# A four-layer network on one core: the rotary part of the query swapped by transfers within SBUF

## The chip, the core and the metric

One Trainium2 chip, one of its cores. The metric is the device time of one execution in microseconds (us); the kernel before was timed three times.

## The reference

Four residual layers over x of shape (4, 512, 1024) in float32: a small attention over the batch, a routed LoRA projection, latent attention with 32 heads, and a second LoRA projection. The change lies in the third. Cut to what matters there:

```python
q = _rmsnorm(x @ wq_a.T, q_a_ln_w) @ wq_b.T            # 32 heads of 64 + 64
q_nope, q_pe = (q[..., :NOPE], q[..., NOPE:])
q_pe = _apply_rope(_deinterleave(q_pe), cos, sin)      # x * cos + rotate_half(x) * sin
k_pe = _apply_rope(_deinterleave(k_pe), cos, sin)
scores = einsum('bqhd,bkhd->bhqk', q_full, k_full) * softmax_scale, causal
out = einsum('bhqk,bkhd->bqhd', softmax(scores), v) @ wo.T
```

`rotate_half` takes the 64 rotary numbers of a head, moves the upper 32 into the place of the lower 32 with a minus sign, and the lower 32 into the place of the upper.

## The kernel before

The heads are worked through as 128 **units**: four groups of eight heads, in each group the four batches, in each batch the eight heads (`units`, L708). A unit has its query transposed: 128 partitions, of which 0 to 63 hold the plain part (with the key's weights already multiplied in) and 64 to 127 the rotary part, by 512 tokens.

Unit u runs through these steps, and the loop at L1214 has several units in work at once:

- `query` (L713): six TensorE matmuls into the PSUM tile `psq` (`po` for the first two units).
- `rotate_query` (L725): ScalarE copies the PSUM tile to `qf` in SBUF (L728). VectorE multiplies the upper 32 rotary partitions of the PSUM tile by the sine into the lower 32 of `t2` (L730), and the lower 32 into the upper 32 (L731). GpSimd multiplies the rotary half of `qf` by the cosine in place (L732), and adds `t2` (L733).
- `split_query` (L736): VectorE rounds 384 tokens of `qf` to the matmul's number format, `qh` (L740), and GpSimd subtracts that from `qf`, `ql` (L741).
- `scores` (L897): for four blocks of queries, TensorE multiplies `qh` and `ql` with the keys into the two PSUM tiles `pss` (L150 to L152 with `ql` first, L912 for the first block), VectorE adds the causal mask and takes the minimum (L918), ScalarE takes the exponential (L921).
- `turn` (L933): TensorE transposes (L942), ScalarE and VectorE copy (L944). `context` (L947): 16 matmuls into `psv` for two units (L958), divided on VectorE (L961) by numbers that `divisors` (L877) sends to DRAM and back: four transfers of 1 KB (L887), two of 64 partitions (L891).
- Between these steps lies filler: `project` (L1007), the output product of the batch before, with its loads (L1020), its splits into two parts (L992 on ScalarE, L993 on GpSimd), its sums (L984, VectorE) and its stores (L1039); and in the first batch of each group `prepare_output` (L1051), which makes the group's output weights (L1068 to L1098).

The query of unit u + 2 is made and rotated in turn u of the loop, split in turn u + 1, used in turn u + 2. All transfers are issued from SyncE's queue (SP), in one order. A planner lays out each engine's order from the program's order and its own estimates; at run time every engine, SP too, works its order strictly in sequence, and an instruction that waits holds those behind it. `qf`, `qh` and `ql` have two buffers each, `t2` has one, `psq` one.

Of the kernel before, what the change touches and what calls it, by code (L numbers as in the profile page):

```python
# [9 lines left out]
F32 = mybir.dt.float32  # L10
FR = mybir.dt.float32r
AF = mybir.ActivationFunctionType
ALU = mybir.AluOpType
# [4 lines left out]
P = 128  # L18
NB, S, D = 4, 512, 1024
# [5 lines left out]
H, NOPE, ROPE, VD, KVR, QR = 32, 64, 64, 128, 64, 256  # L25
# [21 lines left out]
def block_kernel(ctx: ExitStack, tc: tile.TileContext, a: dict, out: bass.AP):  # L47
    nc = tc.nc
    V, A, G, T = nc.vector, nc.scalar, nc.gpsimd, nc.tensor
# [400 lines left out]
    def split_shared(pool, ch):  # L450
# [7 lines left out]
             if kind[0] == "b" and (s or kind == "b11")]  # L458
    w1_d = {(kind, s): dram.tile([P, 2 - ((kind, s) in whole), ND // 2, W1B], F32,
                                 name=f"w1_{kind}{s}") for kind in KINDS for s in range(2)}  # L460
# [48 lines left out]
    with tc.tile_pool(name="b_hTh", bufs=2) as hTh, \  # L509
# [59 lines left out]
        for s, t in enumerate(order):  # L569
# [39 lines left out]
            if s in (10, 11, 12, 13):  # L609
                kind, half = whole[s - 10]  # L610
                row, col = int(kind[1]) - 1, int(kind[2]) - 1
                at = (2 * half + col) * W1B
                with tc.issue_after(kept_x.ins):
                    nc.sync.dma_start(out=w1_d[kind, half][:, 0],
                                      in_=a["w1"][row * ND // 2 : (row + 1) * ND // 2, :, at : at + W1B]
# [26 lines left out]
    cc = attn.enter_context(tc.tile_pool(name="c_const", bufs=1))  # L642
    wqp = attn.enter_context(tc.tile_pool(name="c_wq", bufs=2))
    inp = attn.enter_context(tc.tile_pool(name="c_in", bufs=2))
    qp = attn.enter_context(tc.tile_pool(name="c_q", bufs=2))


    ropeT = cc.tile([P, 2, S], F32, name="ropeT")
    nc.sync.dma_start(out=ropeT[NOPE:P], in_=a["ropeT"])

    causal = cc.tile([P, S], F32, name="causal")
    G.memset(causal, 0.0)
# [58 lines left out]
    lo_, hi_, mid = slice(NOPE, NOPE + 32), slice(NOPE + 32, P), slice(NOPE, P)  # L711
# [13 lines left out]
    def rotate_query(u):  # L725
        ps = queries[u]
        f = qp.tile([P, S], F32, name="qf")
        A.copy(f, ps)  # L728
        t2 = qp.tile([P, S], F32, name="t2", bufs=1)
        V.tensor_tensor(t2[lo_], ps[hi_], ropeT[hi_, 1, :], ALU.mult)  # L730
        V.tensor_tensor(t2[hi_], ps[lo_], ropeT[lo_, 1, :], ALU.mult)  # L731
        G.tensor_tensor(f[mid], f[mid], ropeT[mid, 0, :], ALU.mult)  # L732
        G.tensor_tensor(f[mid], f[mid], t2[mid], ALU.add)  # L733
        queries[u] = f

    def split_query(u):  # L736
# [8 lines left out]
    with tc.tile_pool(name="c1_w", bufs=1, side="right") as wap, \  # L745
# [73 lines left out]
        for s in range(NT + 1):  # L819
            if s < NT:  # L820
                qk[s] = project(s, hts[s])
            if s + 2 < NT:
                hts[s + 2] = turn1(s + 2, ptp)
            if s > 0:
                keep(s - 1, qk[s - 1])
                if order1[s - 1] == TPB - 1:
                    batches[0, 0] = load_batch(0, 0)
            if s in (6, 10):
                wq_raw = fetch_query(s // 4 - 1)
            if s in (8, 12):  # L830
                wqs[s // 4 - 2] = prepare_query(wq_raw, pwp)
            if s in (NT - 2, NT - 1):
                query(s - NT + 2, pwp, "po")
                rotate_query(s - NT + 2)
            if s == NT - 1:
                split_query(0)

                with tc.issue_after(scaled[0].ins):
                    A.activation(first, first, AF.Exp)
# [5 lines left out]
    with ExitStack() as c2:  # L845
# [368 lines left out]
        for u in range(NU + 3):  # L1214
# [37 lines left out]
            if u + 2 < NU:  # L1252
                rotate_query(u + 2)
# [398 lines left out]
def _cos_sin(seq_len, dim=ROPE, base=10000.0, factor=128.0, beta_fast=32.0, beta_slow=1.0,  # L1652
             orig_max=2048):
    import numpy as np

    def corr_dim(r):
        return dim * math.log(orig_max / (r * 2 * math.pi)) / (2 * math.log(base))

    low = max(math.floor(corr_dim(beta_fast)), 0)
    high = min(math.ceil(corr_dim(beta_slow)), dim - 1)  # L1660
    hi = high + 0.001 if low == high else float(high)
    ramp = np.clip((np.arange(dim // 2, dtype=np.float32) - low) / (hi - low), 0.0, 1.0)
    keep = 1.0 - ramp
    extra = 1.0 / base ** (np.arange(0, dim, 2, dtype=np.float32) / dim)
    inter = extra / factor
    inv_freq = inter * (1.0 - keep) + extra * keep
    freqs = np.outer(np.arange(seq_len, dtype=np.float32), inv_freq)
    emb = np.concatenate([freqs, freqs], axis=-1)
    return np.cos(emb).astype(np.float32), np.sin(emb).astype(np.float32)


def _laid_out(i):

    import numpy as np

    even_odd = np.concatenate([np.arange(0, ROPE, 2), np.arange(1, ROPE, 2)])
    half = ROPE // 2
    cos, sin = _cos_sin(S)
    by_tile = lambda t: t.reshape(TPB, P, ROPE).transpose(1, 0, 2)
    signed = np.concatenate([-sin[:, :half], sin[:, half:]], axis=1)  # L1680

    signed_T = np.concatenate([sin[:, :half], -sin[:, half:]], axis=1)
    wkv_a = i["L1_attn_wkv_a"]
    wq_b = i["L1_attn_wq_b"].reshape(H, NOPE + ROPE, QR)
    wkv_b = i["L1_attn_wkv_b"].reshape(H, NOPE + VD, KVR)
    chunks = lambda w: w.T.reshape(ND, P, -1)
    lora_in = lambda w: w.reshape(ER, D)
    lora_out = lambda w: w.transpose(0, 2, 1).reshape(ER, D)
    return {
        "x": i["L0_attn_x"].reshape(NB * S, D),  # L1690
        "w0": chunks(np.concatenate([lora_in(i["L0_ffn_A"]), i["L0_ffn_W_gate"], i["L0_ffn_W_base"]])),
        "b0T": lora_out(i["L0_ffn_B"]),
        "b0": i["L0_ffn_b_base"],
        "waT": chunks(np.concatenate([i["L1_attn_wq_a"], wkv_a[:KVR], wkv_a[KVR:][even_odd]])),
        "q_ln": i["L1_attn_q_a_ln_w"],
        "kv_ln": i["L1_attn_kv_a_ln_w"],
        "wqn": wq_b[:, :NOPE].transpose(1, 0, 2),
        "wqpT": wq_b[:, NOPE:][:, even_odd].transpose(2, 0, 1).reshape(2, P, H, ROPE).transpose(1, 0, 2, 3),
        "wk": wkv_b[:, :NOPE].transpose(1, 0, 2),
        "wv": wkv_b[:, NOPE:].transpose(1, 0, 2),  # L1700
        "woT": i["L1_attn_wo"].T.reshape(H, VD, D),
        "w1": chunks(np.concatenate([i["L1_ffn_W"][:W1B], lora_in(i["L1_ffn_A"]), i["L1_ffn_W"][W1B:]])),
        "b1T": lora_out(i["L1_ffn_B"]),
        "b1": i["L1_ffn_b"],
        "rwT": i["L1_ffn_router_W"].reshape(E, ND, P).transpose(2, 0, 1),
        "rb": i["L1_ffn_router_b"],
        "ropeN": np.stack([by_tile(cos), by_tile(signed)], axis=1),
        "ropeT": np.stack([cos.T, signed_T.T], axis=1),
    }


# [18 lines left out]
```

## Time and profile before

| what | value |
|---|---|
| median of three runs | 1747.93 us (1747.41 to 1749.18) |
| span of the profiled execution | 1746.3 us |
| the stage of the heads in it | about 414 to 1480 us |
| granted TensorE clock, mean | 0.999 |
| ScalarE busy | 905.0 us (52%) |
| L728, copy of the query from PSUM, 126 of 128 | 73.9 us, 587 ns each |
| L730 and L731, 32 x 512, 126 of 128 | 87.7 and 87.1 us, 696 and 691 ns each |
| L732 and L733, 64 x 512, 128 each | 164.4 and 164.3 us, 1285 and 1284 ns each |
| transfers, mean over the span | 131 GB/s, 39.2% of the 16 DMA engines |

Busy time is that of the whole span. The times of the runs lie 1.6 us above the span, since a run has a little before its first instruction and after its last. Line numbers are those of the kernel before.

### The profile page before, as it was taken

What the parts mean: (1) busy time and instruction counts of PE and PEld (TensorE: products, weight loads), DVE (VectorE), ACT (ScalarE), POOL (GpSimd) and SP (SyncE); (2) the same over time, 40 slices, a digit from 0 to 9 for tenths busy, and PEclk for the clock granted to TensorE, in tenths of its full rate; (3) what the DMA queues carried; (4) which work ended last, traced back from release to release, by engine and by line L of the source; (5) the groups of instructions that cost most, each with busy time, mean ns of one, the idle gap of its engine ahead of it and who ended that gap; (6) DMA issues with size and microseconds to landing.
All of it is one profiled execution on the core that took longest, in us unless ns stands there. A gap on an engine that the chain in (4) does not pass through costs nothing.

```text
span 1746.3 us, 31628 instructions
## 1 busy us (share of the span) xinstructions
PE 1707.5 (98%) x10536; PEld 1429.7 (82%) x10536; DVE 1302.4 (75%) x3494; ACT 905.0 (52%) x2316; POOL 921.9 (53%) x926
## 2 busy tenths in 40 slices
PE   7999999999999999999999999999999999999999
PEld 6899999998677777767777767777767777789998
DVE  7977885676777777787777687777778776687675
ACT  7422331366765555575555575555476555453332
POOL 0553541203665665566566556566556655675454
PEclk9999999999999999999999999999999999999999
DMA  4313543245334234353333353342454333853431
GB/s 194 135 42 115 185 159 114 89 138 169 106 99 140 81 118 140 113 172 117 110 112 119 110 193 95 106 139 94 131 169 151 102 110 109 309 201 123 137 105 74
DMA packets 131939, 228.16 MB, mean 131 GB/s; under 512 B 22272, under 2 KB 58752, under 8 KB 128448
## 3 DMA queue, kind: packets, MB, share of 16 engines
q1 hardware_dynamic: 131776, 226.13, 39.2%
q8 instruction: 84, 1.38, 0.3%
q14 instruction: 79, 0.65, 0.1%
HBM read 156.60 MB, written 71.83 MB: 131 GB/s over the span
## 4 chain that ended last, share of the span: by engine, by line
PE 88%; DVE 5%; POOL 4%; ACT 2%; issue 1%; DMA 0%; POOLq 0%; ACTq 0%; DVEq 0%
PE psv L958 8%; PE pst L942 7%; PE po L150 4%; PE po L152 4%; PE po L151 4%; PE pss L150 4%; PE pss L151 3%; PE pss L152 3%; PE pob L150 3%; PE poa L150 3%; PE psq L150 3%; PE psq L152 3%; PE psq L151 3%; PE acc L150 3%; PE acc L152 3%; PE acc L151 3%
## 5 line engine op out<-in xcount | busy, mean ns | idle before, releaser
L921 ACT ACTIVATE p<-p,mn 128x512 f32<-128x512 f32 (+3 forms) x512 | 284.9, 559 | 211.4 <-DVE mn L918 210.8
L732 POOL TENSOR_TENSOR qf<-qf,ropeT 64x512 f32<-64x512 f32 x128 | 164.4, 1285 | 259.1 <-ACT qf L728 249.3
L918 DVE CUSTOM_DVE_ANT_0 p<-pss,causal 128x512 f32<-128x512 f32 (+3 forms) x512 | 232.7, 485 | 19.8 <-PE pss L152 15.8
L942 PE MATMUL pst<-ident,p 128*128 128x128 f32 x1280 | 185.9, 273 | 1.8 <-ACT pT L944 1.7
L733 POOL TENSOR_TENSOR qf<-qf,t 64x512 f32<-64x512 f32 x128 | 164.3, 1284 | 32.0 <-DVE t L731 23.8
L942 PEld LDWEIGHTS pst<-ident,p 128*128 128x128 f32 x1280 | 153.0, 141 | 29.6 <-ACT pT L944 4.8
L944 ACT COPY pT<-pst 128x512 f32<-128x512 f32 x256 | 142.1, 579 | 31.4 <-PE pst L942 29.5
L741 POOL TENSOR_TENSOR ql<-qf,qh 128x384 fp32r<-128x384 f32 x128 | 129.6, 1013 | 53.0 <-DVE qh L740 53.0
L150 PE MATMUL pss<-kT,ql 128*128 128x512 f32 (+2 forms) x384 | 143.6, 374 | 4.4 <-POOL ql L741 4.2
L993 POOL TENSOR_TENSOR cxl<-s,cxh 128x256 fp32r<-128x256 f32 x128 | 98.1, 773 | 85.2 <-ACT cxh L992 53.9
L150 PE MATMUL po<-w_h,hTl 128*128 128x384 f32 (+1 forms) x384 | 133.1, 347 | 0.7 <-DVE x L433 0.6
L151 PE MATMUL pss<-kT,qh 128*128 128x512 f32 (+2 forms) x384 | 130.4, 340 | 0.0
L152 PE MATMUL po<-w_h,hTh 128*128 128x384 f32 (+1 forms) x384 | 130.1, 339 | 0.0
L152 PE MATMUL pss<-kT,qh 128*128 128x512 f32 (+2 forms) x384 | 129.9, 338 | 0.0
L151 PE MATMUL po<-w_l,hTh 128*128 128x384 f32 (+1 forms) x384 | 129.7, 338 | 0.0
L944 DVE COPY pT<-pst 128x256 f32<-128x256 f32 x128 | 54.1, 423 | 97.8 <-PE pst L942 97.2
L728 ACT COPY qf<-psq 128x512 f32<-128x512 f32 x126 | 73.9, 587 | 69.7 <-PE psq L152 68.0
L730 DVE TENSOR_TENSOR t<-psq,ropeT 32x512 f32<-32x512 f32 x126 | 87.7, 696 | 24.5 <-ACT qf L728 20.2
L921 ACT ACTIVATION_READ_ACCUMULATOR p<-p,mn 128x1 f32 x512 | 97.2, 190 | 0.0
L150 PEld LDWEIGHTS pss<-kT,ql 128*128 128x128 f32 x384 | 72.1, 188 | 29.1 <-POOL ql L741 9.2
L731 DVE TENSOR_TENSOR t<-psq,ropeT 32x512 f32<-32x512 f32 x126 | 87.1, 691 | 1.7
L1035 DVE TENSOR_TENSOR xs<-xs,pob 128x512 f32<-128x512 f32 x105 | 71.1, 677 | 19.0 <-PE pob L152 18.8
(567 smaller groups left out, 4975.0 us busy)
## 6 DMA issues: line engine op xcount, KB each, us to landing
xs<-x_d SPq DMA_DIRECT2D x128, 256.0 KB
x_d<-xs SPq DMA_DIRECT2D x128, 256.0 KB
slotC<-in_woT_dram SPq DMA_DIRECT2D x32, 512.0 KB
rb<-r_d SPq DMA_DIRECT2D x128, 128.0 KB
w_t<-raw SPq DMA_DIRECT2D x32, 288.0 KB
x<-in_x_dram SPq DMA_DIRECT2D x16, 512.0 KB
x_d<-x SPq DMA_DIRECT2D x32, 256.0 KB
slotA<-q_d SPq DMA_DIRECT2D x8, 1024.0 KB
```

Source lines behind the costliest of these rows:

```text
L150: T.matmul(ps, lhsT=al, rhs=bh, start=start, stop=False, **kw)
L151: T.matmul(ps, lhsT=ah, rhs=bl, start=False, stop=False, **kw)
L152: T.matmul(ps, lhsT=ah, rhs=bh, start=False, stop=stop, **kw)
L732: G.tensor_tensor(f[mid], f[mid], ropeT[mid, 0, :], ALU.mult)
L733: G.tensor_tensor(f[mid], f[mid], t2[mid], ALU.add)
L741: G.tensor_tensor(l, f[:, P:S], f32(h), ALU.subtract)
L918: turn_of[0] = V.tensor_tensor_reduce(out=to, in0=ps[:, 0:n], in1=causal[:, S - n : S], scale=1.0, scalar=-NEG, op0=ALU.add, op1=ALU.min, ...
L921: A.activation(to, to, AF.Exp, bias=mn[:, i : i + 1], scale=-1.0, accum_out=rs[:, i : i + 1])
L942: T.transpose(ps[:, w : w + P], p[:, OF[i] + j * P : OF[i] + (j + 1) * P], ident)
L944: copy(pT[:, AT[js[0]] : AT[js[0]] + w], ps[:, 0:w])
L958: T.matmul(ps[n * KVR : (n + 1) * KVR, S - w : S], lhsT=k[:, j, :], rhs=pTs[u + n][:, AT[j] : AT[j] + w], start=(j == 0), stop=(j == TPB - 1))
L993: G.tensor_tensor(l, src, f32(h), ALU.subtract)
```

## The change

The query's rotary half is rotated from SBUF. After ScalarE's copy, two transfers carry 32 partitions by 512 numbers each (64 KB) of `qf` into partitions 0 to 63 of `t2`, crosswise. VectorE multiplies these 64 partitions by the signed sine in one instruction, into partitions 64 to 127 of `t2`. GpSimd multiplies by the cosine into a tile of its own, `tc`, and adds. The table `ropeT` has the signed sine in partitions 0 to 63 and the cosine in 64 to 127, 2 KB a partition where it had 4 KB in half the partitions.

```diff
-    ropeT = cc.tile([P, 2, S], F32, name="ropeT")
-    nc.sync.dma_start(out=ropeT[NOPE:P], in_=a["ropeT"])
+    ropeT = cc.tile([P, S], F32, name="ropeT")
+    nc.sync.dma_start(out=ropeT, in_=a["ropeT"])
...
         A.copy(f, ps)
         t2 = qp.tile([P, S], F32, name="t2", bufs=1)
-        V.tensor_tensor(t2[lo_], ps[hi_], ropeT[hi_, 1, :], ALU.mult)
-        V.tensor_tensor(t2[hi_], ps[lo_], ropeT[lo_, 1, :], ALU.mult)
-        G.tensor_tensor(f[mid], f[mid], ropeT[mid, 0, :], ALU.mult)
-        G.tensor_tensor(f[mid], f[mid], t2[mid], ALU.add)
+        nc.sync.dma_start(out=t2[0:32], in_=f[hi_])
+        nc.sync.dma_start(out=t2[32:NOPE], in_=f[lo_])
+        V.tensor_tensor(t2[mid], t2[0:NOPE], ropeT[0:NOPE], ALU.mult)
+        tc_ = qp.tile([P, S], F32, name="tc", bufs=1)
+        G.tensor_tensor(tc_[mid], f[mid], ropeT[mid], ALU.mult)
+        G.tensor_tensor(f[mid], tc_[mid], t2[mid], ALU.add)
         queries[u] = f
...
-    signed_T = np.concatenate([sin[:, :half], -sin[:, half:]], axis=1)
...
-        "ropeT": np.stack([cos.T, signed_T.T], axis=1),
+        "ropeT": np.concatenate([signed.T, cos.T]),
```

## The prediction

> **What bounds the kernel now.** I read the page first, then the busy time by stretches, then the timeline unit by unit, last the waits.
>
> ```profile
> PE 1707.5 (98%) x10536; PEld 1429.7 (82%) x10536; DVE 1302.4 (75%) x3494; ACT 905.0 (52%) x2316; POOL 921.9 (53%) x926
> ...
> DMA  4313543245334234353333353342454333853431
> ...
> PE 88%; DVE 5%; POOL 4%; ACT 2%; issue 1%; DMA 0%; POOLq 0%; ACTq 0%; DVEq 0%
> ```
>
> TensorE (PE) is busy all along and makes 88% of the chain that ended last. VectorE and GpSimd (POOL) hold 5% and 4% of it, 87 and 70 us: places, not the whole.
>
> ```profile
> 414.00:500.00 86.00, 80.87 (x445) 56.11 (x444) 67.00 (x197) 61.67 (x167) 55.19 (x49) 1.00 0.45 145
> 500.00:620.00 120.00, 120.00 (x675) 94.32 (x674) 87.76 (x242) 67.59 (x189) 71.93 (x71) 1.00 0.31 101
> ```
>
> Columns: stretch, its length, busy PE, weight loads, VectorE, ScalarE, POOL, clock, share of the DMA engines, GB/s. In the steady stretch TensorE has no idle time at a clock of 1.00: shorter work elsewhere can give nothing back there, a late operand can only take. The start of the heads has 5 us of idle TensorE in 86.
>
> How late may the operand come? One unit, from its query to its score:
>
> ```profile
> 608.99 0.59 ACT L728 COPY qf<-psq 128x512 f32<-128x512 f32 x1 [0.53 <-PE psq L152]
> ...
> 609.67 0.70 DVE L730 TENSOR_TENSOR t<-psq,ropeT 32x512 f32<-32x512 f32 x1
> 609.72 1.28 POOL L732 TENSOR_TENSOR qf<-qf,ropeT 64x512 f32<-64x512 f32 x1 [0.70 <-ACT qf L728]
> ...
> 610.38 0.69 DVE L731 TENSOR_TENSOR t<-psq,ropeT 32x512 f32<-32x512 f32 x1
> ...
> 611.21 1.28 POOL L733 TENSOR_TENSOR qf<-qf,t 64x512 f32<-64x512 f32 x1 [0.21 <-DVE t L731]
> ...
> 612.52 0.36 DVE L740 CAST qh<-qf 128x384 fp32r<-128x384 f32 x1 [0.25 <-POOL qf L733]
> ...
> 612.96 1.01 POOL L741 TENSOR_TENSOR ql<-qf,qh 128x384 fp32r<-128x384 f32 x1 [0.47 <-DVE qh L740]
> ```
>
> The copy ends at 609.58 (call it E), the two multiplications end at E + 1.49, the cosine at E + 1.42, the addition runs from E + 1.63 to E + 2.91, `ql` is done at 613.97. In the timeline the first weight load of this unit's scores comes at 617.27: 3.3 us to spare. The unit before it has nothing to spare:
>
> ```profile
> 608.01 1.01 POOL L741 TENSOR_TENSOR ql<-qf,qh 128x384 fp32r<-128x384 f32 x1
> ...
> 609.07 0.19 PEld L150 LDWEIGHTS pss<-kT,ql 128*128 128x128 f32 x1
> ```
>
> Reading all 128 units so, from the end of L741 to that weight load, I count 39 units with under 0.35 us, 16 with 0.35 to 1.3, 15 with 1.3 to 2.4, 58 with more. The 39 are of two kinds. Some 20 lie in the steady stretch, as the one above: its addition ended at 604.57, but L740 had its turn on VectorE only at 606.31 and L741 its turn on POOL, behind three L993, at 608.01; so 1.7 us of lateness vanish before L741, except what the L993 between are pushed. The other 19 lie in the start of the heads (units 0 to 11) and in the three later stretches of `prepare_output`, with the addition, L740, L741 and the scores end to end. The waits say the same in sum:
>
> ```profile
> PEld pss L150 <- POOL ql L741: 9.2, 23, 1.5
> ```
>
> **The change, part by part.** *VectorE:* 128 x (0.696 + 0.691) = 177 us go, and one multiplication over 64 partitions comes. Its price is not in the trace; nearest is L984, two SBUF inputs, 128 x 512:
>
> ```profile
> L984 DVE TENSOR_TENSOR s<-a,a x16: 679/811/1328, 1506.8 to 1718.0; 128x512 f32<-128x512 f32 x16
> ```
>
> So 0.68 to 1.33 us; I take 0.75, as POOL has mostly just ended the cosine. The spread comes from POOL, as this pair shows (another L984, 128 x 256, takes 0.41 undisturbed at 605.38):
>
> ```profile
> 757.66 1.01 POOL L741 TENSOR_TENSOR ql<-qf,qh 128x384 fp32r<-128x384 f32 x1 [0.47 <-DVE qh L740]
> ```
>
> ```profile
> 757.84 1.10 DVE L984 TENSOR_TENSOR s<-cx 128x256 f32<-128x256 f32 x1
> ```
>
> The removed multiplications read PSUM and never stretch (695 to 697 ns in all 128). The Trainium skill ("SBUF — State Buffer", section "SBUF: two separate sides") has here an exclusive lock: a VectorE operation with two SBUF inputs and a GpSimd operation that reads SBUF each hold the other out for the whole instruction. The row ends 0.27 us after POOL's, less than a full 0.41, so the lock is not quite that strict; by the rule a multiplication that meets a whole GpSimd operation would cost 0.69 + 1.28 = 1.97 us, an estimate, and such a meeting alone would make its unit's lateness 2.5 where I take 1.3.
>
> VectorE is thus relieved by 128 x (1.387 - 0.75) = 82 us of busy time. I cost this at nothing, because the steady stretch is TensorE's; where VectorE is on the chain it is a gain, in the rivals. `psq` comes free when the copy ends, 1.4 us earlier; TensorE waited for that once, 0.5 us.
>
> *Transfers:* 256 of 64 KB, 16.8 MB on 226 MB, 7%: not the bandwidth. What counts is issue and landing, and the trace shows no transfer within SBUF. Nearest are the four of 1 KB to DRAM, whose landing the next two wait for:
>
> ```profile
> 599.82 1.30 SPq L887 DMA_DIRECT2D r_d<-rt  x4
> ...
> 602.54 1.09 SPq L891 DMA_DIRECT2D rb<-r_d  x2
> ```
>
> An issue costs 1.30 / 4 = 0.33 us, and from the end of the last issue (601.12) to 602.54 are 1.42 us. So the second swap is issued by E + 0.05 + 0.66 and has landed at E + 2.1 with a free queue. Bounds: 0.7 less if a landing within SBUF takes half; and more when it waits its turn: SP gives 1.30 + 1.09 us to the divisors every second unit, and loads wait on SP for earlier transfers with all behind them held:
>
> ```profile
> SPq L1020 <- DMA x_d<-xs: 61.9, 60, 3.4
> ```
>
> or when the 16 engines still work off 1 MB of loads (a load of 256 KB at the steady 101 GB/s over a share of 0.31, some 325 GB/s, takes 0.8 us, four 3.2). The Trainium skill ("DMA: Bandwidth & Descriptors", section "Anatomy of one DMA") gives 2.0 us plus the bytes over 436 GB/s, for GpSimd's path: 2.15 us for 64 KB, and its rules for kernel authors advise against small transfers and against halving one by partitions. By it, as an estimate, landing is at E + 2.9 and every shift below is 0.8 larger, some 36 us more in the sum; I hold to the row, which is of the same queue.
>
> *POOL:* same two operations of 1.28 us; the new tile changes no wait, since only POOL touches it before the addition. `ropeT` is the same 256 KB once: nothing.
>
> *The shift.* Multiplication from E + 2.1 to E + 2.85, addition from E + 2.9 where it was E + 1.6: **1.3 us later** (0.6 with the quick landing; 1.9 with the stretched multiplication; 2.4 to 3.0 behind the divisors' issues or loads).
>
> *What 1.3 us costs.* I move each addition in the timeline, push POOL's operations behind it, L740 and L741 as far as needed, and count what comes after the scores' weight load. The 19 tight units pay 0.1 to 1.3, 0.55 in the mean (several have 0.3 to 1.7 us between addition and L740): 10 us. The 20 steady ones pay what the L993 were pushed, 0.2: 4 us. All others have room. Sum 14 us for an unhindered transfer. The same count gives 27 us at a shift of 1.6, 41 at 1.9, 66 at 2.4, 105 at 3.0, and 3 at 0.7. For hindered transfers I add 5 us: about one unit in eight meets a queue of a further 1.1 us and pays some 0.3 of it beyond its slack, 16 x 0.3.
>
> VectorE's multiplication itself waits for the transfer. Behind it stand L918, the copies L944 and L740, hence ScalarE's exponential and TensorE's transposes. I cost that wait at nothing because VectorE idles 32 of 120 us in the steady stretch, 2 us a unit, if the planner sets the multiplication at its due time; where it does not, that is the first rival. Swaps waiting on SP for the copy hold `r_d` and loads behind them for well under 1 us; `rb` is due some 8 us later.
>
> Sum: span 1746.3 + 14 + 5 - 1 (VectorE's relief, `psq`) = 1764.3; the median stands 1.6 above the span: **1766 us**. The likeliest case's own range, shifts of 1.0 to 2.1 (6 to 50 us): 1754 to 1798.
>
> **The rivals.** *Late transfers block VectorE.* SP's order and the load queue bring a swap 3 us late in the mean and VectorE stands in front of L918. For: SP's waits, the DMA slices at 4 to 8 tenths; against: at 3 tenths most swaps meet a free queue. By the count, 105 us: 1853; it decides from a mean landing of E + 3.8, and half as much (2.4, 66 us) still ends at 1814.
>
> *The lateness is hidden.* The planner sees the transfer and moves the filler of `project` ahead of the scores, so that tight units stop being tight. For: 73 of 128 units have over 1.3 us; against: the start has little filler and the tight places are bound by POOL. Then only some 2 us remain: 1749.
>
> *VectorE's relief wins.* In the start of the heads the chain of waits gives 3.2% of 86 us to L731 and about 2% to L730; 0.64 us less a unit for the 45 or so units outside the steady stretch, at a third of them on the chain, is 10 us: 1738. It decides if a swap lands before E + 0.7, since the addition is then no later; half the row's landing and a joined issue would be needed. Against: 1.42 us for 1 KB.
>
> *The change does not do what it says:* a multiplication stretched to 1.33 by POOL leaves VectorE as busy as before (1.39); that is the shift of 1.9 above, inside the forecast.
>
> **How the numbers follow.** Forecast 0.58, blocked VectorE 0.16, hidden 0.13, relief 0.13. A measurement tells 0.2% (3.5 us) from no change. Slower holds the first two, 0.74; the hidden case is the same, 0.13; relief faster, 0.13. From 1743 to 1805 leaves about 0.1 out below and 0.1 above.
>
> **What would show it.** After: the addition starts 2.9 us behind the copy's end, not 1.6; `pss` weight loads wait for `ql` some 25 us in sum, not 9; the new multiplication lasts 0.69 alone and longer beside POOL; TensorE's work is the same with more idle time between 414 and 500 and in the three stretches of `prepare_output`. I am wrong if TensorE's idle time sits in front of transposes (late exponentials: blocked VectorE), or if the addition comes no later.

## The result, and the profile after

| kernel | median, range | ratio to before, 95% interval |
|---|---|---|
| before | 1748.33 us (1747.41 to 1749.18) | |
| after | 1925.66 us (1923.63 to 1929.21) | 1.1015 [1.1002, 1.1029] |

The change costs 177 us. The prediction had the side right and the size wrong: 1766 us, with a range that ended at 1805.

From the page of the kernel after, the busy time of the engines, TensorE's (PE) share and its granted clock by slices, and the groups of VectorE's mask instruction (L920), of the scores' first matmuls (L150), of the addition (L735), of the new multiplication (L732) and of the context's division (L963) (behind the bar: mean ns of one, then idle time in front of the group and what ended it):

```profile
PE 1751.6 (91%) x10536; PEld 1452.1 (75%) x10536; DVE 1236.4 (64%) x3366; ACT 908.3 (47%) x2316; POOL 932.9 (48%) x926
...
PE   7999999998888999978999978999997988989999
...
PEclk9999999999899999989999999999998999999999
...
L920 DVE CUSTOM_DVE_ANT_0 p<-pss,causal 128x512 f32<-128x512 f32 (+3 forms) x512 | 234.7, 488 | 189.8 <-PE pss L152 177.4
L150 PE MATMUL pss<-kT,ql 128*128 128x512 f32 (+2 forms) x384 | 150.5, 392 | 136.7 <-POOL ql L743 136.6
L735 POOL TENSOR_TENSOR qf<-tc,t 64x512 f32<-64x512 f32 x128 | 164.6, 1286 | 148.3 <-DVE t L732 79.0
...
L732 DVE TENSOR_TENSOR t<-t,ropeT 64x512 f32<-64x512 f32 x128 | 106.3, 831 | 16.9 <-DMA t<-qf 13.3
...
L963 DVE TENSOR_TENSOR cx<-psv,rb 128x512 f32<-128x512 f32 x64 | 44.2, 691 | 79.1 <-PE psv L960 71.9
```

TensorE has the same 10536 matmuls, and where it was busy 98% of the span it is busy 91%. VectorE (DVE) has 66 us less to do, as the change means it to, and that is worth nothing. The main cause stands in the line of L150: 136.6 us in which TensorE waits for `ql`, the last product of the query's chain (4.2 before). The addition, further up that chain, waits 79.0 us for the multiplication; this is GpSimd's idle time and no further part of the loss.

The span grew by 178 us: TensorE is idle 134 us longer, and it is also busy 44 us longer (1707.5 before) with the same matmuls. The granted clock shows where part of the 44 comes from. In the slices it is 9 all through before; here it is 8 in three of them, and its mean is 0.983 where it was 0.999. By the clock's records 68 us of the span run at half clock (5 before), and TensorE is busy in 54 of them (3 before): some 26 us more work time, as an estimate. The remaining 18 are not broken down. What lowers the clock no run shows by itself; the runs with much idle time on TensorE have it (of the runs below, 39 us at half clock in `unread`, 67 in `order`), those with little have not (2 in `unread_const`, 5 in `deep_swap`). So the prices below hold TensorE's waits and the lower clock together.

The stretches that the prediction showed, of the kernel after (same columns):

```profile
414.00:500.00 86.00, 70.02 (x342) 47.52 (x341) 43.32 (x141) 48.18 (x130) 38.98 (x34) 0.94 0.41 124
500.00:620.00 120.00, 105.56 (x572) 79.18 (x571) 71.24 (x199) 60.63 (x169) 65.85 (x63) 0.99 0.33 102
```

The steady stretch, 120.00 of 120 before, now has 14 us of idle TensorE. All but some 3 us of the loss is in the heads: the first copy of a query ends at 415.2 us (414.6 before), and from the last copy to the end it is 280.4 us (277.8).

One unit in the timeline of the kernel after, from its copy to its scores (start, length; the copy ends at 641.82, which is E):

```profile
641.23 0.59 ACT L728 COPY qf<-psq 128x512 f32<-128x512 f32 x1 [0.69 <-POOL ql L743]
...
642.30 0.51 SPq L730 DMA_DIRECT2D t<-qf  x1
...
642.86 0.59 SPq L731 DMA_DIRECT2D t<-qf  x1
...
645.32 0.69 DVE L1037 TENSOR_TENSOR xs<-xs,pob 128x512 f32<-128x512 f32 x1 [0.34 <-PE pob L152]
...
645.93 0.42 DVE L920 CUSTOM_DVE_ANT_0 p<-pss,causal 128x256 f32<-128x256 f32 x1
...
646.38 1.14 DVE L732 TENSOR_TENSOR t<-t,ropeT 64x512 f32<-64x512 f32 x1
...
647.65 1.29 POOL L735 TENSOR_TENSOR qf<-tc,t 64x512 f32<-64x512 f32 x1 [0.68 <-POOL cxl L995]
...
649.41 0.99 POOL L743 TENSOR_TENSOR ql<-qf,qh 128x384 fp32r<-128x384 f32 x1 [0.47 <-DVE qh L742]
...
650.46 0.50 PE L150 MATMUL pss<-kT,ql 128*128 128x512 f32 x1 [1.43 <-POOL ql L743]
```

SyncE (SP) starts the first swap 0.48 us behind the copy, since it is still issuing the divisors' transfers; the two issues last 0.51 and 0.59 us; the second swap's semaphore moves at 644.84 (E + 3.0). VectorE doesn't take up the multiplication then: two instructions stand ahead of it, and the first of them waits for TensorE (0.34 us). The multiplication starts at E + 4.6, the addition at E + 5.8, and TensorE stands 1.43 us in front of the scores.

Over all 128 units (means from the instructions' own times):

| behind the copy's end | predicted | measured, mean (median) |
|---|---|---|
| first swap's issue starts | 0.05 | 1.02 (0.25) |
| second swap's issue ends | 0.71 | 2.29 (1.64) |
| both have landed | 2.1 | 3.95 (3.28) |
| multiplication starts | 2.1 | 6.07 (5.40) |
| addition starts | 2.9 | 7.28 (6.32) |

Between the landing and the multiplication lie 2.1 us in the mean, 271 us over all units. In these VectorE works 142 us and stands idle for 129, 118 of them in front of instructions that wait for TensorE, the divisions of L963 (57 us) and L920 (50) above all. So TensorE's own lateness comes back through VectorE's order: late scores make those instructions late, and they hold the next multiplication.

Before, the addition started at 1.84 (1.58). Units with under 0.35 us between `ql` and the scores' weight load were 39; they are 117.

### The profile page after: what moved, and what is told of

Read it like the earlier page. It is cut to its first block, busy times and chain, and to the rows that moved or that the text cites. A ratio compares the mean times of both kernels' runs of the same rounds, so it can differ in the third digit from the quotient of the medians.

```text
span 1924.4 us, 32100 instructions
## 1 busy us (share of the span) xinstructions
PE 1751.6 (91%) x10536; PEld 1452.1 (75%) x10536; DVE 1236.4 (64%) x3366; ACT 908.3 (47%) x2316; POOL 932.9 (48%) x926
## 5 line engine op out<-in xcount | busy, mean ns | idle before, releaser
L920 DVE CUSTOM_DVE_ANT_0 p<-pss,causal 128x512 f32<-128x512 f32 (+3 forms) x512 | 234.7, 488 | 189.8 <-PE pss L152 177.4
L150 PE MATMUL pss<-kT,ql 128*128 128x512 f32 (+2 forms) x384 | 150.5, 392 | 136.7 <-POOL ql L743 136.6
L735 POOL TENSOR_TENSOR qf<-tc,t 64x512 f32<-64x512 f32 x128 | 164.6, 1286 | 148.3 <-DVE t L732 79.0
L150 PEld LDWEIGHTS pss<-kT,ql 128*128 128x128 f32 x384 | 75.9, 198 | 183.6 <-POOL ql L743 166.4
L734 POOL TENSOR_TENSOR tc<-qf,ropeT 64x512 f32<-64x512 f32 x128 | 167.7, 1310 | 80.5 <-ACT qf L728 74.3
L995 POOL TENSOR_TENSOR cxl<-cx,cxh 128x256 fp32r<-128x256 f32 x96 | 72.2, 755 | 140.4 <-ACT cxh L994 137.9
L151 PE MATMUL pss<-kT,qh 128*128 128x512 f32 (+2 forms) x384 | 136.4, 355 | 0.0
L152 PE MATMUL pss<-kT,qh 128*128 128x512 f32 (+2 forms) x384 | 135.7, 353 | 0.0
L150 PE MATMUL po<-w_h,hTl 128*128 128x384 f32 (+1 forms) x384 | 133.0, 346 | 0.2 <-DVE x L433 0.2
L742 DVE CAST qh<-qf 128x384 fp32r<-128x384 f32 x128 | 46.1, 360 | 127.6 <-POOL qf L735 127.6
L732 DVE TENSOR_TENSOR t<-t,ropeT 64x512 f32<-64x512 f32 x128 | 106.3, 831 | 16.9 <-DMA t<-qf 13.3
L963 DVE TENSOR_TENSOR cx<-psv,rb 128x512 f32<-128x512 f32 x64 | 44.2, 691 | 79.1 <-PE psv L960 71.9
```

The costliest lines, as they stand in the source:

```text
L150: T.matmul(ps, lhsT=al, rhs=bh, start=start, stop=False, **kw)
L151: T.matmul(ps, lhsT=ah, rhs=bl, start=False, stop=False, **kw)
L152: T.matmul(ps, lhsT=ah, rhs=bh, start=False, stop=stop, **kw)
L732: V.tensor_tensor(t2[mid], t2[0:NOPE], ropeT[0:NOPE], ALU.mult)
L734: G.tensor_tensor(tc_[mid], f[mid], ropeT[mid], ALU.mult)
L735: G.tensor_tensor(f[mid], tc_[mid], t2[mid], ALU.add)
```

## The experiments

The theory after the result: the loss is the lateness of the addition; it comes from SP's queue, from the issues, and from the place that the multiplication has in VectorE's order. The rivals: the transfers' own traffic, the hold-up between VectorE's multiplication, which now reads SBUF alone, and GpSimd, and a VectorE that stands waiting for transfers. Unless said otherwise a diff is against the kernel after.

**Are the transfers as such the cost?** Two runs keep both transfers and take VectorE's products from PSUM again. In `unread` the transfers land where nobody reads them, though GpSimd's addition, which writes into `qf`, still has to wait until they have read it:

```diff
-        V.tensor_tensor(t2[mid], t2[0:NOPE], ropeT[0:NOPE], ALU.mult)
+        V.tensor_tensor(t2[lo_], ps[hi_], ropeT[0:32], ALU.mult)
+        V.tensor_tensor(t2[hi_], ps[lo_], ropeT[32:NOPE], ALU.mult)
```

> The changed kernel with its transfers kept, but nobody waits for them: they land in partitions 0 to 63 of t2, which nothing reads, and VectorE makes the two products from PSUM as before (the cosine product stays in its own tile). Theory A, lateness (the rotated query reaches the scores late, since the addition starts 7.3 us behind the copy in the mean instead of some 1.9): 1748 to 1760 us, the addition back under 2.5 us behind the copy. Theory B, load (256 more transfers on the one queue and the DMA engines hold up others): 1800 us or more.

Measured: 1843.64 us, ratio 1.054 [1.0525, 1.0556]; the addition starts at 4.51 (us behind the copy's end, mean, as all such numbers below). From the waits of `unread` (time in all, number, longest):

```profile
POOL qf L736 <- DMA t<-qf: 63.5, 40, 4.6
...
PE pss L150 <- POOL ql L744: 57.5, 46, 5.2
```

The addition still waits for a transfer, and TensorE for the addition's chain. So this run did not free the chain, and it can't price the traffic. In `unread_const` the transfers read the constant table in place of `qf`:

```diff
-        nc.sync.dma_start(out=t2[0:32], in_=f[hi_])
-        nc.sync.dma_start(out=t2[32:NOPE], in_=f[lo_])
+        nc.sync.dma_start(out=t2[0:32], in_=ropeT[hi_])
+        nc.sync.dma_start(out=t2[32:NOPE], in_=ropeT[lo_])
```

(with VectorE's two lines as in `unread`)

> Like the run unread, but the 256 transfers read the constant rope table instead of qf, so that nothing waits for them at all (in unread the addition into qf still waited until the transfers had read it); both products from PSUM. Traffic and issues on SP alone. If they cost by themselves: 1775 us or more. If the cost is the lateness of the addition: 1748 to 1760 us, the addition under 2.5 us behind the copy.

Measured: 1756.95 us, 1.0054 [1.004, 1.0068]; addition at 1.86. The same 256 transfers of 64 KB, issued from the same queue, cost 9 us when nothing waits for them. The traffic falls as a cause of 177 us. One thing this run leaves out: its transfers read a constant, so they are issued 5.5 us ahead of the copy's end in the mean and SP never stands for a copy. In the change SP does:

```profile
SPq L730 <- ACT qf L728: 185.1, 69, 8.1
SPq L889 <- DVE rt L885: 137.9, 34, 9.0
```

The loads and stores behind such a wait are held. In the change TensorE's own waits for loads in the heads are 1.2 us in sum, and VectorE's for `rb` 6.8, so little of the loss lies there. `act_queue` below takes the swaps off SP.

**The multiplication alone, without transfers.** `no_transfer` multiplies `qf` in SBUF straight on; `psum64` multiplies the PSUM tile. Both leave out the swap of the halves and take the cosine for the sine.

```diff
-        nc.sync.dma_start(out=t2[0:32], in_=f[hi_])
-        nc.sync.dma_start(out=t2[32:NOPE], in_=f[lo_])
-        V.tensor_tensor(t2[mid], t2[0:NOPE], ropeT[0:NOPE], ALU.mult)
+        V.tensor_tensor(t2[mid], f[mid], ropeT[mid], ALU.mult)
```

> The changed kernel without its two transfers: one product over 64 partitions from SBUF, of the rows as they stand (the swap of the halves is left out). Theory A: 1740 to 1752 us, as the product follows the copy at once; VectorE has 0.7 us less a unit. Theory C, the product from SBUF costs by itself, since it and GpSimd hold each other up: 1770 us or more, with the product well over 0.83 us in the mean.

Measured: 1780.6 us, 1.0176 [1.0159, 1.0193].

In `psum64` the added line is:

```diff
+        V.tensor_tensor(t2[mid], ps[mid], ropeT[mid], ALU.mult)
```

> Like the run no_transfer (one product over 64 partitions, halves not swapped, no transfer), but the product reads PSUM instead of qf, so that only one of its inputs is in SBUF. If the 31 us of no_transfer come from VectorE and GpSimd holding each other up: 1742 to 1752 us, with the cosine product at 1.28 us where it was 1.72. If they come from another order of the work or from the separate cosine tile: 1770 to 1785 us again.

Measured: 1747.27 us, 0.9996 [0.9986, 1.0005]. VectorE is relieved by some 0.69 us a unit, 88 us in sum, and the kernel doesn't move: the relief is worth nothing here. And one operand from SBUF in place of PSUM costs 33 us. The timeline of `no_transfer` shows how:

```profile
849.75 0.69 DVE L730 TENSOR_TENSOR t<-qf,ropeT 64x512 f32<-64x512 f32 x1
849.86 1.72 POOL L732 TENSOR_TENSOR tc<-qf,ropeT 64x512 f32<-64x512 f32 x1 [1.85 <-ACT qf L728]
```

GpSimd's (POOL) cosine product starts beside VectorE's and lasts 1.72 us; its mean is 1.68 here and 1.29 in `psum64`. In the 107 units where VectorE starts first and undisturbed, its product still has 0.59 us to run when GpSimd's starts, and GpSimd's is 0.46 us longer. From the waits of `no_transfer`:

```profile
PE pob L150 <- POOL cxl L993: 12.1, 14, 1.6
PE poa L150 <- POOL cxl L993: 10.3, 13, 0.9
```

TensorE waits 22.4 us for GpSimd's other work, the low parts `cxl` of the output product's operand, 3.7 us before (2.9 and 0.8) and 1.9 in `psum64`. So most of this loss, some 20 of the 33 us, goes by GpSimd's time and not by the query, whose addition starts at 2.11. The kernel after hardly has it: there the multiplication comes when the cosine product is long done, that one lasts 1310 ns in the mean, and TensorE's waits for `cxl` stay at 3.5 us. So hardly any of the 33 us is in the 177.

**Which part of the lateness?** `act_queue` issues the transfers from ScalarE's own queue, right behind the copy:

```diff
-        nc.sync.dma_start(out=t2[0:32], in_=f[hi_])
-        nc.sync.dma_start(out=t2[32:NOPE], in_=f[lo_])
+        nc.scalar.dma_start(out=t2[0:32], in_=f[hi_])
+        nc.scalar.dma_start(out=t2[32:NOPE], in_=f[lo_])
```

> The changed kernel with the two transfers issued from ScalarE's queue, right behind the copy, instead of SP's. If SP's order holds the swaps up (first issue 1.0 us behind the copy in the mean, up to 9.7): 1870 to 1910 us, with issues right behind the copy. If ScalarE's own issues (256 of some 0.55 us) put the exponentials late: 1930 us or more.

Measured: 1887.75 us, 1.0811 [1.0779, 1.0843]. The first issue starts at 0.14 (1.02 in the change), the landing is at 3.58, the addition at 6.03. 38 us of the 177 come back, so SP's order is not the main part. Nor are the 38 its price alone: the landing is only 0.4 us earlier, and 0.9 us of the addition's 1.25 come from a shorter stand of the multiplication behind the landing (1.2 us for 2.1), while ScalarE now spends 0.58 us on each of the 256 issues. `one_transfer` moves the 64 partitions in one piece, its halves not swapped:

```diff
-        nc.sync.dma_start(out=t2[0:32], in_=f[hi_])
-        nc.sync.dma_start(out=t2[32:NOPE], in_=f[lo_])
+        nc.sync.dma_start(out=t2[0:NOPE], in_=f[mid])
```

> The changed kernel with one transfer of 64 partitions by 512 in place of two of 32 (the swap of the halves is left out). If the second issue on SP (0.55 to 0.59 us) and its semaphore are a share: landing some 0.6 us earlier, the addition 0.6 to 1.3 us earlier, 1885 to 1910 us. If the landing and the order alone set it: 1915 to 1930 us.

Measured: 1883.8 us, 1.0775 [1.076, 1.079]; landing at 3.38, addition at 5.79. One transfer in place of two is worth 42 us, again by two ways: the landing is 0.6 us earlier, and the multiplication stands 1.15 us behind it in place of 2.1. `swap_product` lets VectorE multiply from PSUM at once (the table's sine is signed for the place that the product goes to), and swaps the product's halves afterwards, so that only GpSimd's addition waits for a transfer:

```diff
-        nc.sync.dma_start(out=t2[0:32], in_=f[hi_])
-        nc.sync.dma_start(out=t2[32:NOPE], in_=f[lo_])
-        V.tensor_tensor(t2[mid], t2[0:NOPE], ropeT[0:NOPE], ALU.mult)
-        tc_ = qp.tile([P, S], F32, name="tc", bufs=1)
-        G.tensor_tensor(tc_[mid], f[mid], ropeT[mid], ALU.mult)
-        G.tensor_tensor(f[mid], tc_[mid], t2[mid], ALU.add)
+        V.tensor_tensor(t2[mid], ps[mid], ropeT[0:NOPE], ALU.mult)
+        t3 = qp.tile([P, S], F32, name="t3", bufs=1)
+        nc.sync.dma_start(out=t3[lo_], in_=t2[hi_])
+        nc.sync.dma_start(out=t3[hi_], in_=t2[lo_])
+        G.tensor_tensor(f[mid], f[mid], ropeT[mid], ALU.mult)
+        G.tensor_tensor(f[mid], f[mid], t3[mid], ALU.add)
```

> One product over 64 partitions straight from PSUM behind the copy (sine signed for the place that it goes to), then the two transfers swap the halves of the product, and GpSimd adds what has landed: correct rotation, no VectorE operation behind the transfer, no two SBUF inputs on VectorE, the cosine product in place. If the place of the product in VectorE's order (2.1 us behind the landing in the mean) is a share of the loss: the addition at 3.5 to 4.8 us behind the copy and, at some 30 us per us of lateness, 1800 to 1850 us. If whatever comes behind a transfer is set so late on its engine, GpSimd too: the addition at 6 us or more, 1880 to 1930 us.

Measured: 1855.65 us, 1.0616 [1.0602, 1.0631]. The landing is later than in the change, 4.55, because the multiplication comes first; still the addition is earlier, 5.90, and 70 us come back. A transfer behind the multiplication is cheaper than one ahead of it. `order` tried the place itself: VectorE's context and filler of the next turn were put behind the multiplication (`turned_q[0]` is that instruction).

```diff
-            advance(cx)
-            advance(filler, per[0])
+            with tc.issue_after(turned_q[0].ins):
+                advance(cx)
+                advance(filler, per[0])
```

> The changed kernel, with the next turn's context and filler work on VectorE queued behind the rotary product, so that the product stands earlier in VectorE's order. Of theory A, if the place in the order (2.1 us behind the landing in the mean) is the larger share: the product within 1 us of the landing, the addition some 1.5 to 2 us earlier, 1830 to 1880 us. If the transfer's own 3 us are the share that counts: 1900 to 1940 us, and VectorE waits for the transfer in front of the product.

Measured: 1954.49 us, 1.1173 [1.1154, 1.1193]: a miss, and slower than the change. The multiplication still starts 2.0 us behind the landing in the mean (2.1 in the change), the addition at 6.97, and the work that was put behind it is late as well (TensorE waits 11.7 us for the sums `xs` of the output product, 0.4 in the change). The edit moved other work without moving the multiplication much, so it says nothing of what a better place would bring.

**A longer lead.** `deep_after` makes the query three units ahead in place of two. Room for a third `qf` comes from one of five `xs` tiles and one of two `junk` tiles.

```diff
-        f = qp.tile([P, S], F32, name="qf")
+        f = qp.tile([P, S], F32, name="qf", bufs=3)
...
-            if 0 < u < NU - 2:
-                query(u + 2, psq, "psq")
-            if u + 2 < NU:
-                rotate_query(u + 2)
+            if 0 < u < NU - 3:
+                query(u + 3, psq, "psq")
+            if u + 3 < NU:
+                rotate_query(u + 3)
```

> The changed kernel, transfers and all, but the query of unit u + 3 instead of u + 2 is made and rotated in turn u, with a third buffer for qf (room for it: four instead of five xs tiles, one junk tile): some 8 us more between rotation and split. Theory A: most of the 177 us come back, 1750 to 1790 us, with TensorE's wait for ql under 60 us in sum where it was 303. Theory B or C: no less than 1880 us, since load and lock stay the same.

Measured: 1773.26 us, 1.0136 [1.0121, 1.0151]. The addition starts at 6.95, nearly as late as in the change, and yet 152 of the 177 us are gone; 20 units are tight in place of 117, and the clock is at half for 14 us in place of 68. The multiplication stands 1.2 us behind the landing in place of 2.1, though `rotate_query` stands at the same place of the loop. So the lateness is paid only where a unit has no slack for it. The same lead on the kernel before is `deep_before`:

> The kernel before with the same deeper lead as deep_after (query of u + 3, three qf buffers, four xs tiles, one junk tile). Control of deep_after: what it lies below 1773 us is the change's own cost when there is time for it. If the 20 or so units before that had nothing to spare cost anything: 1735 to 1745 us; if the smaller room costs: 1750 to 1765 us.

Measured: 1746.12 us, 0.9989 [0.998, 0.9999]. The lead itself gives almost nothing, for the kernel before has little lateness to hide.

What are the 27 us that `deep_after` lies above `deep_before`? The theory then was the hold-up of `no_transfer`. Three runs with the longer lead (`deep_no_transfer` and `deep_swap_sbuf` take the cosine for the sine, and the first leaves out the swap): `deep_swap` is `swap_product` with it, `deep_no_transfer` is `no_transfer` with it, and `deep_swap_sbuf` is `deep_after` with these lines:

```diff
-        nc.sync.dma_start(out=t2[0:32], in_=f[hi_])
-        nc.sync.dma_start(out=t2[32:NOPE], in_=f[lo_])
-        V.tensor_tensor(t2[mid], t2[0:NOPE], ropeT[0:NOPE], ALU.mult)
+        V.tensor_tensor(t2[0:NOPE], f[mid], ropeT[mid], ALU.mult)
+        nc.sync.dma_start(out=t2[lo_], in_=t2[32:NOPE])
+        nc.sync.dma_start(out=t2[hi_], in_=t2[0:32])
```

> The longer lead of deep_after (the query three units ahead, three qf buffers, four xs tiles, one junk buffer) with the rotation of swap_product: VectorE multiplies all 64 partitions from PSUM, where the product shares no lock with GpSimd (psum64: no loss), and two transfers then swap the product's halves before GpSimd's addition. It asks what the 27 us are that deep_after still lies above deep_before. If they are the hold-up between VectorE's product from SBUF and GpSimd's cosine product (no_transfer against psum64: 31 us), this run is at 1750 to 1760: deep_before and the 9 us that the transfers cost by themselves in unread_const. If they are lateness that three units of lead don't cover, or the transfers' own load, it is at 1768 or above, as deep_after is at 1773. In both cases far below swap_product (1856), and the addition still starts 5 to 6 us behind the copy's end.

Measured: 1748.26 us, 1.000 [0.999, 1.001], a little under the hold-up theory's own number.

> no_transfer with the longer lead of deep_after: VectorE's one product reads qf in SBUF beside GpSimd's cosine product, nothing waits for a transfer. It leaves out the swap of the halves and multiplies by the cosine in place of the sine. If the 27 us that deep_after lies above deep_before come from the hold-up between VectorE's product from SBUF and GpSimd, as deep_swap's 1748 suggests, they are here too: 1765 to 1780. If the longer lead covers the hold-up as it covers deep_swap's transfers, because 0.44 us a unit are small against a median slack of some 8 us, it is at 1746 to 1752, and the 27 us belong to the place that VectorE's product has behind a transfer.

Measured: 1746.9 us, 0.9986 [0.9977, 0.9996], though the cosine product still lasts 1.67 us in the mean. The theory falls: with this lead the hold-up costs nothing.

> deep_swap with VectorE's product taken from qf in SBUF in place of PSUM (and GpSimd's cosine product into a tile of its own, as in the change); the two transfers swap the product's halves as there. It multiplies by the cosine in place of the sine. Hold-up theory: deep_swap and some 25 us, 1768 to 1780. Theory of VectorE's product queued behind a transfer: it isn't queued behind one here, so 1748 to 1755, as deep_swap.

Measured: 1770.87 us, 1.0122 [1.0105, 1.0139]. By its number this run would speak for the hold-up; its waits show something else as well. TensorE's waits in the heads, of `deep_after`, then `deep_swap`, then `deep_swap_sbuf`:

```profile
PE pss L150 <- POOL ql L743: 27.3, 15, 3.4
```

```profile
PE pss L150 <- POOL ql L743: 4.9, 6, 1.1
```

```profile
PE pss L914 <- DVE mn L920: 7.9, 5, 2.4
PE pss L150 <- DVE mn L920: 7.3, 8, 1.2
PE pss L150 <- POOL ql L743: 6.7, 6, 1.5
PE pob L150 <- DVE xs L1037: 6.1, 5, 1.4
```

and VectorE's own wait in front of its multiplication in `deep_swap_sbuf`:

```profile
DVE t L730 <- POOL qf L735: 15.3, 11, 2.4
```

In `deep_after` it is `ql` again, 27.3 us in 15 waits: single units with more lateness than even this lead covers. In `deep_swap` that has shrunk to 4.9. `deep_swap_sbuf` waits for VectorE instead, and it has an edit too many: product and swapped product share the one buffer of `t2`, so that VectorE's multiplication stood 15.3 us for GpSimd's addition of the unit before, with VectorE's other work behind it. That wait is new; how much of the 23 us is its own and how much the hold-up's was not taken apart.

**The version that beats both.** `deep_table` is the kernel before with the longer lead and with the packed table of the change, whose 2 KB a partition leave room for all five `xs` tiles (the diff is against the kernel before):

```diff
-        V.tensor_tensor(t2[lo_], ps[hi_], ropeT[hi_, 1, :], ALU.mult)
-        V.tensor_tensor(t2[hi_], ps[lo_], ropeT[lo_, 1, :], ALU.mult)
-        G.tensor_tensor(f[mid], f[mid], ropeT[mid, 0, :], ALU.mult)
+        V.tensor_tensor(t2[lo_], ps[hi_], ropeT[0:32], ALU.mult)
+        V.tensor_tensor(t2[hi_], ps[lo_], ropeT[32:NOPE], ALU.mult)
+        G.tensor_tensor(f[mid], f[mid], ropeT[mid], ALU.mult)
```

> The kernel before with the deeper lead, but all five xs tiles: the rope table is packed as in the changed kernel (sine in partitions 0 to 63, read beside PSUM rows 64 to 127), which makes room for the third qf buffer. Rotation from PSUM, no transfer. If the units that before had nothing to spare cost something that the four xs tiles of deep_before took back: 1736 to 1744 us. If TensorE's own work is all there is to it: 1745 to 1750 us.

Measured: 1742.27 us (1739.27 to 1746.4), 0.9964 [0.9953, 0.9975]: 6 us faster than the kernel before, with no transfers.

## Why the prediction was wrong

**The failed step is the shift of the addition**, "1.3 us later". Measured it is 7.28 - 1.84 = 5.4 us in the mean. Its pieces, which are not independent, since lateness feeds back through VectorE's order:

- *The landing*, put at E + 2.1, was at 3.95. The tail behind the last issue, 1.42 us from the divisors' row, was right: it measured 1.44 in the median. But an issue of 32 x 512 lasts 0.57 us and not the 0.33 of a 1 KB transfer (0.5 us on two). And SP isn't free: the first issue starts 1.02 us behind the copy in the mean, which the prediction put at 0.05 and let grow only for one unit in eight. The median is 0.25; the mean comes from some units that wait up to 9.7 us, behind divisors, the output weights' loads (L1048, held up to 5.5 us for TensorE) and the addition of the unit before, which holds the one `t2`.
- *The place on VectorE* was costed at nothing "if the planner sets the multiplication at its due time". It doesn't: the multiplication starts 2.1 us behind the landing in the mean, only 17 of 128 within 0.2 us of it. Its idle time in the group's line is 16.9 us, 13.3 of it for the transfer, so it hardly ever stands for the transfer itself: it stands behind other instructions, which VectorE works for 142 us and waits to begin for 129, mostly for TensorE. The prediction's 2 us a unit of idle VectorE were counted where TensorE had no late operand. That the planner's own estimate of the landing sets this place was not shown. `swap_product`, which takes the multiplication out from behind the transfer, wins 70 us.
- *The multiplication*, taken at 0.75 us, lasted 0.83, a small error; the addition then starts 0.38 us behind its end, where 0.05 was taken.

**What a shift costs** was counted unit by unit, and that curve held for moderate shifts. Between its 66 us at 2.4 and 105 at 3.0, a shift of 2.7 would be some 85; `unread`, shifted by 4.51 - 1.84 = 2.7, lost 95. The count ends there. Carried on with its last slope, 65 us for each microsecond, it would say 170 at 4.0 and 260 at 5.4, an estimate; three runs near 4.0 lost 107 to 139, and the change 177:

| run | addition starts, mean | over before |
|---|---|---|
| before | 1.84 | 0 |
| unread | 4.51 | 95 |
| one_transfer | 5.79 | 135 |
| swap_product | 5.90 | 107 |
| act_queue | 6.03 | 139 |
| after | 7.28 | 177 |
| deep_before | 1.95 | -2 |
| deep_swap | 5.88 | 0 |
| deep_after | 6.95 | 25 |

With two units of lead, 26 to 36 us are paid for each microsecond of mean lateness, the lower clock included. The count moved each unit alone, where a late unit holds TensorE and so gives the next one time; that this is why it overshoots is argued, not shown. The clock was taken as 1.00 throughout, which the profile before gave no reason to doubt; some 26 us of the loss come with its fall.

The likeliest case's own range, "1754 to 1798", leaves out the prediction's own +5 and -1; the measured time lies far above it either way.

**The steady stretch** was to pay almost nothing, since TensorE was full there and most units had room. That follows from the shift: the median slack before was 1.7 us, and 5.4 us exceed it. The prediction's own count would have said so at the right shift.

**VectorE's relief** at nothing was right, and `psum64` shows it. The rival "VectorE's relief wins" falls with it. "The lateness is hidden" falls for the kernel as it is; it is what `deep_swap` makes of it.

**"Late transfers block VectorE"** came nearest, 1853 us from a mean landing of E + 3.8; the landing was 3.95. Its mechanism did not happen: VectorE stands in front of that instruction (L920 after) for TensorE, 177.4 us, and in front of the multiplication for a transfer only 13.3 us; TensorE's idle time lies in front of the scores for `ql` and not in front of the transposes. It had the landing right and lacked the 2.1 us behind it.

**The two rules that the prediction cited.** The Trainium skill's "DMA: Bandwidth & Descriptors", section "Anatomy of one DMA", gave 2.15 us for 64 KB, as an estimate; here one issue and its tail are 0.57 + 1.44 = 2.01 us, so its sum (landing at E + 2.9) came nearer to an unhindered swap than the row's 2.1: the 66 units whose first issue starts within 0.35 us of the copy's end have a median landing of 2.69. The same page's advice against halving a transfer by partitions (section "Rules for kernel authors") agrees with `one_transfer`, 42 us. The exclusive lock of the skill's "SBUF — State Buffer", section "SBUF: two separate sides", shows in `no_transfer` nearly whole: 0.46 us on GpSimd's 1.29 where VectorE's instruction had 0.59 us left to run. With an operand from PSUM (`psum64`) it doesn't show.

**The signs named beforehand:** the addition at 2.9 came at 7.28; the scores' weight loads wait 166.4 us for `ql` in place of 25; the multiplication is 0.68 us alone and up to 1.28 beside GpSimd, as said.

## What to carry to other kernels

A transfer put into a chain costs more than issue and landing: add the issuing queue's lateness and the place of the instruction behind it, which in a planned order can come well after the landing, and compare that sum with the slack of every unit. An engine that then waits makes the instructions behind it late too, so the lateness can grow round the loop, and here the clock fell with it. Where the chain needs the transfer, put engine work that can go first ahead of it and start the chain a whole unit earlier: the swaps that cost 107 us with two units of lead cost nothing measurable with three. Relief of an engine that isn't what TensorE waits for can be worth nothing: here 88 us of it were.

## What the hardware showed that was not expected

- The issue of a 32 x 512 transfer within SBUF holds SP for 0.57 us in the mean (0.51 at the least, single ones up to 1.56), nearly twice a 1 KB transfer to DRAM (0.33), and its landing, 1.44 us behind the issue's end in the median, is no quicker than that one's 1.42. One transfer of 64 x 512 has an issue of 0.49 us and lands 1.77 behind it.
- 16.8 MB moved by 256 transfers beside a full TensorE cost 9 us in all when nothing waits for them.
- In the change TensorE's granted clock is at half for 68 us, in stretches of 3.4 or 6.8 us, where it was for 5 before.
- A VectorE product with both inputs in SBUF lengthens a GpSimd product beside it by 0.4 us (1.29 to 1.68); with one input in PSUM by nothing.
